# The scan layer's first and last steps: earlier row loads, a first scan inside the convolution, and the last norm, tokens and output products laid into the steps

## The chip, the core and the metric

The kernel runs on one core of one Trainium2 chip. The metric is device time in microseconds (us) from one launch, and smaller is better. Four engines compute: TensorE (PE, with weight loads shown as PEld), VectorE (DVE), ScalarE (ACT) and GpSimd (POOL). Nearly all transfers are issued from SyncE's queue (SP). All data are float32.

## The reference, cut to what matters

Four layers change x (3 images, 256 channels, 48 x 48 pixels), each in the form x + layer(norm(x)), where norm is a group norm over 32 groups. Layer 0 holds attention, layers 1 and 2 are 3 x 3 convolutions, and layer 3 is a selective state-space scan. The change lies between layers 2 and 3 and at the end of layer 3:

```
x = x + conv3x3(group_norm(x))            # layer 2
xn = layer_norm(group_norm(x))            # layer 3, tokens of 256 channels
x_in, z = split(xn @ in_proj.T)           # 512 + 512
u = silu(causal_conv(x_in, 4 taps))
dt_raw, Bm, Cm = split(u @ x_proj.T)      # 16 + 16 + 16
dt = softplus(dt_raw @ dt_proj.T + bias)
h_t = h_(t-1) * exp(dt_t * A) + dt_t * u_t * Bm_t    # 512 x 16 states
y_t = sum_n(h_t * Cm_t) + u_t * D
x = x + (y * silu(z)) @ out_proj.T
```

## The kernel before, in words

**Layer 2.** `output` takes one half image and one half of its channels. PE makes six products (`products`, L1546), ACT copies some of them (L1562), DVE combines them and adds them to the image in SBUF (L1564 to L1576). The images are taken in the order 2, 1, 0, so image 0 (tile x0) is written last, and its very last write is one L1576 on DVE. Finished halves are copied by ACT into token order and stored to DRAM (`store_tokens`, L1642 and L1649), since layer 3 takes its chunks from there. The group norm of a finished image is made in small steps (`next_norm`, `norm_steps`, L183 to L195, L216 to L218, L1614). Beside this the generator `early_preparation` already prepares layer 3's chunk 0 and part of chunk 1: one step of it runs after each product. It ends with dt and dt*u of chunk 0 stored to DRAM (`keep_dt`, L1353 and L1355), and z projected (L1359, L1367).

**Layer 3.** The tokens are cut into 18 chunks of 384 (six for each image). A chunk takes 8 steps, (m, h) for m = 0..3 and h = 0, 1, so there are 144 steps. A step holds eight scans of 128 x 385 on DVE (`scan`, L1819), in parts 0 to 7; each one runs along the tokens. What a step needs:

- dt and dt*u spread over the partitions: `spread` (L1714) and `spread_second` (L1722) reload them from DRAM on SP in groups of four DMAs; `spread_pe` (L1730) spreads two rows by PE into PSUM (ps_r).
- the decays exp(dt*A): `decay` (L1811), one ACT instruction for each scan, into three PSUM slots in turn (ps_da), so ACT can be three scans ahead.
- the products dt*u*B that the scan runs over, in tile hs: the upper half by DVE (`fill_upper`, L1765, from ps_r), the rest by POOL (`fill`, L1780 and L1785).
- after the scans POOL multiplies by C (`times_c`, L1836, 128 x 3072; in the last step DVE does it in two halves, L1830), PE adds the states (`add_states`, L1848 and L1853), and after two steps of an m DVE multiplies by silu(z) (`gate`, L1860).

`run` lays the preparation of the next two chunks and the output of the chunk before (`project_y` L1372 and L1374, `store` L1384 and L1385) between the scans at places given by tables. `keep_busy` (L1336) puts idle 128 x 128 products on PE. From the line `mark` on, `keep_order` fixes the written order on PE, DVE, ACT and POOL. SP's order is left to the scheduler.

**The two ends.** At the start, after layer 2's pools are closed, the code loads the first rows (`spread`, `spread_second`, `spread_pe` for chunk 0), copies the first states (L1794), fills, makes three decays and goes into the loop. Before that, DVE makes the four `diag` matrices (L1704), three memsets (L1748), and the last image's statistics and norm. At the end, after the loop, the residual is loaded, `project_y` adds the residual and m = 0..2, then the last states are added, the last gate is made, the products of m = 3 are added, and ACT copies both halves for two stores.

Of the kernel before, what the change touches and what calls it, by code (L numbers as in the profile page):

```python
# [9 lines left out]
F32 = mybir.dt.float32  # L10
I32 = mybir.dt.int32
AF = mybir.ActivationFunctionType
# [72 lines left out]
def net(  # L85
# [36 lines left out]
    def v(name, i=0, n=1):  # L122
        at = VEC_AT[name] + i
        return vec[:, at : at + n]
# [1254 lines left out]
    def residual(k):  # L1379
        k.ot = room(k, "ot")  # L1380
        nc.sync.dma_start(k.ot, xd[k.b][:, :, k.c * CH : (k.c + 1) * CH])

    def store(k, mo):
        nc.scalar.copy(k.ot[:, mo, :], k.y_out[mo])  # L1384
        nc.sync.dma_start(  # L1385
            out[k.b, mo * P : (mo + 1) * P, k.c * CH : (k.c + 1) * CH], k.ot[:, mo, :]
        )
# [68 lines left out]


    def early_preparation():

# [58 lines left out]
        for m in (0, 2):  # L1518
            project_dt(k, m)
            yield  # L1520
            softplus(k, m)
            yield
            take_dt(k, m)
            yield
            keep_dt(k, m)
            yield
        for m in (0, 2):
            for j in range(2):
                project_z(k, m + j, j)
            yield  # L1530
            for j in range(2):
                take_z(k, m + j, j)
            yield


    with ExitStack() as l1:
# [46 lines left out]
        def moments(b):  # L1583
# [17 lines left out]
            return mv  # L1601

        def next_norm(layer, b):

            last = layer and b == ORDER[-1]
            known = None if last else moments(b)
            for _ in range(9):
                yield
            _, sc, sh = yield from group_norm_steps(b, pss, "s", known=known)
            if layer == 0:  # L1610
                norms[b] = sixth(sc, sh)
            else:
                keep = const.tile([P, 2, CT], F32, name=f"norm3{b}")
                nc.vector.tensor_copy(keep[:, 0, :], sc)  # L1614
                nc.vector.tensor_copy(keep[:, 1, :], sh)
                norm3[b] = keep[:, 0, :], keep[:, 1, :]
# [13 lines left out]
        def store_tokens(b, h):  # L1630


            last = (b, h) == (ORDER[-1], 1)
            if last:
                t = vp.tile([P, 6, CT, (HR + 2) * TW], F32, name="vt")
                t = t.rearrange("p i t n -> p (i t n)")
            else:
                t = pad.tile([P, 4, CT * (HR + 2) * PW + 2], F32, name="xpad")
                t = t.rearrange("p j n -> p (j n)")
            t = t[:, : CT * 4 * HN].rearrange("p (t n) -> p t n", t=CT)  # L1640
            for ct in range(CT):
                nc.scalar.copy(  # L1642
                    t[:, ct, :].rearrange("p (n j) -> p j n", j=4),
                    xs[b][:, ct, :].rearrange("p (j n) -> p j n", j=4)[
                        :, :, h * HN : (h + 1) * HN
                    ],
                )
            queue = nc.scalar if last else nc.sync
            queue.dma_start(xd[b][:, :, h * 4 * HN : (h + 1) * 4 * HN], t)  # L1649
            stored.add((b, h))  # L1650
# [3 lines left out]
        for n, (k, h) in enumerate(halves):  # L1654
# [7 lines left out]
            for m in range(2):  # L1662
                output(b, h, m, u, vt, v("l2_bias", 0, 2) if layer else None)
                for _ in range(13):
                    next(beside.get(k, iter(())), None)
                if m == 0 and behind is not None:
                    store_tokens(*behind)
                    behind = None
# [3 lines left out]
            if h == 1:  # L1672
# [3 lines left out]
                next(pending)  # L1676
        store_tokens(*behind)
        for _ in pending:
            pass
        for _ in early:  # L1680
# [8 lines left out]
    with ExitStack() as l3:  # L1689
        wp = l3.enter_context(tc.tile_pool(name="w3", bufs=1, reuse_waits="tile"))  # L1690
        psd = l3.enter_context(tc.tile_pool(name="psd", bufs=1, space=PSUM))
        psr = l3.enter_context(tc.tile_pool(name="psr", bufs=1, space=PSUM))
        psy = l3.enter_context(tc.tile_pool(name="psy", bufs=1, space=PSUM))

        scn = l3.enter_context(tc.tile_pool(name="scn", bufs=2, reuse_waits="tile"))
        for name in ("u", "dtu", "bc0", "bc1", "sz"):
            rooms[name].append(wp.tile([P, 4, CH], F32, name=name))
# [4 lines left out]
        diag = wp.tile([P, DI, P], F32, name="diag")  # L1702
        for m in range(DI):
            nc.vector.tensor_scalar(diag[:, m, :], ident, v("D", m), None, ALU.mult)  # L1704

# [39 lines left out]
        parts_of_step = [(g, q) for a in range(2) for g in range(2) for q in (2 * a, 2 * a + 1)]  # L1745
        slots = [psd.tile([P, 512], F32, name=f"ps_da{i}") for i in range(3)]
        for t in slots:
            nc.vector.memset(t[:, :1], 0.0)  # L1748

        def states(s):  # L1750

            if s not in tiles:
                t = scn.tile([P, 2, 4, CH + 4], F32, name="hs", bufs=3)
                tiles[s] = t[:, :, :, 1 : CH + 2]
            return tiles[s]
# [15 lines left out]
        def fill(s):  # L1771

            at, m, h = steps[s]
            if h == 0:
                fill_upper(s, 0, 2)
                fill_upper(s + 1, 0, 1, 1 if m == DI - 1 else 2)
            else:
# [45 lines left out]
        def times_c(s):  # L1823
            at, m, h = steps[s]
            cb = chunks[at].bc[1][:, 2 * h : 2 * h + 2, :].unsqueeze(2)
            hc = scn.tile([P, 2, 4, CH], F32, name="hc")
            if s == len(steps) - 1:
# [34 lines left out]
        mark = listed[-1]  # L1862
        last = len(todo) - 1
        k = chunks[0]
        k.rows = {0: spread(k, 0)}
        spread_second(k, 0)
        spread_pe(k, 0)
        first_states(0)
        fill(0)
        for n in range(3):  # L1870
            decay(n)
        for s, (at, m, h) in enumerate(steps):
            if m == 0 and h == 1 and at + 2 <= last:
                fetch(at + 2)
            for part in range(8):
                j = 4 * m + 2 * h + part // 4
                scan(s, part)
                decay(8 * s + part + 3)
                if (m, h, part) in busy:
                    g, q = parts_of_step[part]  # L1880
                    keep_busy(tiles[s][:, g, q, 1 : P + 1], busy[m, h, part])
                if part == 0 and h == 0:
# [6 lines left out]
                if part == 4 and s + 1 < len(steps):  # L1889
                    first_states(s + 1)  # L1890
                if part % 4 == 0:
                    run(at, j, BEGIN)
                if part % 4 == 1:
                    run(at, j, MID)
                if part % 4 == 2:
                    run(at, j, DONE)
                if h == 1 and part == 7 and s >= 3:
                    gate(*steps[s - 3][:2])
# [4 lines left out]
            if s + 1 < len(steps):  # L1903
                fill(s + 1)
            last_states(s)
            times_c(s)
# [6 lines left out]

        end = len(steps) - 1
        k = chunks[last]
        residual(k)
        for mo in range(2):
            project_y(k, mo, 0, DI - 1)
        add_states(end)
        gate(*steps[end][:2])  # L1920
        for mo in range(2):
            project_y(k, mo, DI - 1, DI)
            store(k, mo)
        keep_order(tc, listed, mark)
# [113 lines left out]
```

## Time and profile before

| what | value |
|---|---|
| median of 3 runs | 3367.3 us (3366.03 to 3369.35) |
| the profiled execution's own time | 3369.11 us |
| its span, first to last instruction | 3367.4 us |
| granted TensorE clock over the span | 0.978 |
| busy PE, DVE, ACT, POOL | 3159.9, 2892.8, 2376.1, 1346.1 us |
| last layer 2 product begins | 2008.68 us, its last write on DVE at 2011.79 us |
| first scan begins | 2022.25 us |
| last scan ends, last copy of the output ends | 3344.68 us, 3359.48 us |

Times in the text are microseconds from the start of the span of the one profiled execution. A row such as "L1819 DVE ... xN | busy, mean ns" names a source line, its engine, the operation and how often it ran. The chain of waits follows the work that ended last back from the end, so a wait on it is time that counts; a wait off it may cost nothing.

### The profile page before, as it was taken

What the parts mean: (1) busy time and instruction counts of PE and PEld (TensorE: products, weight loads), DVE (VectorE), ACT (ScalarE), POOL (GpSimd) and SP (SyncE); (2) the same over time, 40 slices, a digit from 0 to 9 for tenths busy, and PEclk for the clock granted to TensorE, in tenths of its full rate; (3) what the DMA queues carried; (4) which work ended last, traced back from release to release, by engine and by line L of the source; (5) the groups of instructions that cost most, each with busy time, mean ns of one, the idle gap of its engine ahead of it and who ended that gap; (6) DMA issues with size and microseconds to landing.
All of it is one profiled execution on the core that took longest, in us unless ns stands there. A gap on an engine that the chain in (4) does not pass through costs nothing.

```text
span 3367.4 us, 54979 instructions
## 1 busy us (share of the span) xinstructions
PE 3159.9 (94%) x21314; PEld 1591.0 (47%) x21314; DVE 2892.8 (86%) x3302; ACT 2376.1 (71%) x3596; POOL 1346.1 (40%) x457
## 2 busy tenths in 40 slices
PE   7999999999999999979999997999999999999995
PEld 4334343352333434547777763444444444444442
DVE  3799989958989998369975459999999999999997
ACT  2688888838888886331324447888888888888874
POOL 0000000000000000220000009999999999999997
PEclk9999999999999999989999999999999999999987
DMA  4000000010000002566611135455555555555552
GB/s 165 31 8 10 8 8 6 8 46 5 8 7 8 10 8 71 174 217 216 216 31 38 38 105 122 120 125 131 134 130 140 135 127 128 133 127 137 133 133 56
DMA packets 182164, 290.84 MB, mean 86 GB/s; under 512 B 34737, under 2 KB 148465, under 8 KB 179970
## 3 DMA queue, kind: packets, MB, share of 16 engines
q1 hardware_dynamic: 168658, 267.15, 29.4%
q10 hardware_dynamic: 13232, 20.06, 1.8%
q8 instruction: 169, 2.77, 0.4%
q14 instruction: 105, 0.86, 0.1%
HBM read 236.24 MB, written 50.64 MB: 85 GB/s over the span
## 4 chain that ended last, share of the span: by engine, by line
PE 52%; DVE 32%; ACT 7%; DMA 5%; issue 4%; SPq 1%; POOL 0%; ACTq 0%; DVEq 0%; POOLq 0%
DVE hs L1819 21%; PE ps_s L638 16%; PE acc L651 14%; PE ps_c L1546 8%; DVE hs L1765 3%; PE ps_s L1031 2%; DVE u L296 2%; PE ps_y L462 2%; ACT ps_da L1811 2%; PE ps_m L665 1%; PE ps_m L711 1%; PE acc L529 1%; PE ps_s L518 1%; DVE ps_g L1343 1%; PE ps_s L578 1%
## 5 line engine op out<-in xcount | busy, mean ns | idle before, releaser
L642 ACT ACTIVATE pt<-ps_s 128x1024 f32<-128x1024 f32 x972 | 942.5, 1022 | 154.6 <-PE ps_s L638 142.1
L1819 DVE TENSOR_TENSOR_SCAN hs<-ps_da,hs 128x385 f32<-128x385 f32 x1152 | 1002.1, 935 | 4.2 <-ACT ps_da L1811 1.5
L857 DVE TENSOR_TENSOR part<-part,pt 128x2048 f32<-128x2048 f32 x396 | 906.6, 2289 | 41.2 <-ACT pt L642 18.4
L1811 ACT ACTIVATE ps_da<-dtr,u 128x384 f32<-128x384 f32 x1152 | 656.6, 582 | 184.3 <-DVE hs L1819 175.7
L164 POOL TENSOR_TENSOR rstd<-ve,mhalf 128x2 f32<-128x2 f32 (+1 forms) x26 | 16.3, 629 | 1480.3 <-DVE ve L162 1480.3
L638 PE MATMUL ps_s<-q,kt 32*128 32x512 f32 (+1 forms) x4320 | 576.4, 592 | 0.1
L651 PE MATMUL acc<-pt,vt 128*32 128x512 f32 (+1 forms) x4320 | 520.9, 561 | 0.2
L1546 PE MATMUL ps_c<-vt,u 128*128 128x288 f32 x1728 | 432.4, 411 | 20.6 <-DVE u L263 20.6
L1836 POOL TENSOR_TENSOR hc<-hs,x 128x3072 f32<-128x3072 f32 x72 | 405.3, 5629 | 19.2 <-DVE hs L1819 15.2
L1836 POOL TENSOR_TENSOR hc<-hs,bc 128x3072 f32<-128x3072 f32 x71 | 399.9, 5633 | 15.9 <-DVE hs L1819 14.2
L1546 PEld LDWEIGHTS ps_c<-vt,u 128*128 128x128 f32 x1728 | 330.8, 192 | 117.1 <-issue 19.4
L638 PEld LDWEIGHTS ps_s<-q,kt 32*128 32x128 f32 x4320 | 195.2, 183 | 199.1 <-issue 120.2
L651 PEld LDWEIGHTS acc<-pt,vt 128*32 128x32 f32 x4320 | 94.4, 108 | 353.4 <-issue 326.7
L1853 PE MATMUL ps_y<-hc,u 128*32 128x384 f32 x2304 | 230.4, 521 | 2.8 <-POOL hc L1836 2.8
L1273 PE MATMUL ps_g<-u 128*128 128x384 f32 x576 | 195.2, 491 | 23.5 <-ACT u L1269 23.5
L1785 POOL TENSOR_TENSOR hs<-dtur,x 128x1536 f32<-128x1536 f32 x72 | 209.2, 2905 | 9.1 <-DMA dtur<-dtud 8.5
L1785 POOL TENSOR_TENSOR hs<-dtur,bc 128x1536 f32<-128x1536 f32 x72 | 209.3, 2907 | 1.1 <-DMA dtuq<-dtud 1.1
L1273 PEld LDWEIGHTS ps_g<-u 128*128 128x128 f32 x576 | 108.3, 191 | 107.2 <-ACT u L1269 34.7
L1336 PE MATMUL ps_r<-hs,ident 128*128 128x128 f32 x864 | 130.7, 292 | 19.8 <-DVE hs L1819 19.5
L1336 PEld LDWEIGHTS ps_r<-hs,ident 128*128 128x128 f32 x864 | 107.6, 192 | 73.8 <-DVE hs L1819 56.1
L1853 PEld LDWEIGHTS ps_y<-hc,u 128*32 128x32 f32 x2304 | 62.4, 113 | 145.0 <-issue 129.6
L1562 ACT COPY cb<-ps_c 128x288 f32<-128x288 f32 x48 | 19.2, 399 | 157.5 <-PE ps_c L1546 137.9
(266 smaller groups left out, 4062.8 us busy)
## 6 DMA issues: line engine op xcount, KB each, us to landing
wconv<-in_we SPq DMA_DIRECT2D x144, 384.0 KB, 4.4
dtr<-dtd SPq DMA_DIRECT2D x288, 192.0 KB, 3.9
dtur<-dtud SPq DMA_DIRECT2D x288, 96.0 KB, 4.2
wconv<-xd SPq DMA_DIRECT2D x36, 384.0 KB, 3.7
x<-bcd SPq DMA_DIRECT2D x72, 192.0 KB, 5.0
dtd<-x SPq DMA_DIRECT2D x36, 384.0 KB, 2.9
dtuq<-dtud SPq DMA_DIRECT2D x288, 48.0 KB, 2.0
bc<-bcd SPq DMA_DIRECT2D x72, 192.0 KB, 4.9
```

The source lines that it names most:

```text
L638: nc.tensor.matmul(s[:, j, cols], kt[r, mt * P : (mt + 1) * P], q[r, :n], start=True, stop=True,)
L642: nc.scalar.activation(p[:, h0 : h0 + 2, :], s, AF.Exp)
L651: nc.tensor.matmul(acc[h * HD : (h + 1) * HD, :n], vt[:, mt, g * P + h * HD : g * P + (h + 1) * HD], p[:, h, cols], start=mt == 0, stop=mt ...
L857: ): nc.vector.tensor_tensor(part, first, p, ALU.add)
L1273: nc.tensor.matmul(bank[m % 2], w3v["taps"][:, m, tap, :], w3v["xi"][:, m % 3, tap : tap + CH], start=tap == 0, stop=tap == DCONV - 1,)
L1336: nc.tensor.matmul(spread_tiles[-1][:, i % 2, CH:], ident, src, start=True, stop=True)
L1546: nc.tensor.matmul(pc[:, :HN], u[:, i, dy, ct, m * P : (m + 1) * P], vt[:, i, ct, dy * TW : dy * TW + HN], start=ct == 0 and dy == 0, stop ...
L1785: nc.gpsimd.tensor_tensor(states(s)[:, :, 2:4, 1:], chunks[at].rows[m][1].unsqueeze(1).broadcast_to([P, 2, 2, CH]), b_rows(s, 0, 2), ALU.mult,
L1811: nc.scalar.activation(slots[n % 3][:, 1 : CH + 1], chunks[at].rows[m][0][:, q, :], AF.Exp, scale=amat[:, col : col + 1],)
L1819: nc.vector.tensor_tensor_scan(b, slots[(8 * s + part) % 3][:, : CH + 1], b, 0.0, ALU.mult, ALU.add)
L1836: nc.gpsimd.tensor_tensor(hc, tiles[s][:, :, :, 1:], cb.broadcast_to([P, 2, 4, CH]), ALU.mult)
L1853: nc.tensor.matmul(k.y_ps[32 * q : 32 * q + 32, :CH], fold, hc[:, g, q, :], start=False, stop=h == 1 and g == 1,)
```

## The change

- **First rows.** A new function `first_rows`, called by `early_preparation` after the last `keep_dt`, issues sixteen DMAs for chunk 0, m = 0: the rows for POOL and the two rows for DVE's fill go into the two xg buffers (SBUF instead of PSUM), dt goes into the dt buffer. The `spread`, `spread_second` and `spread_pe` that stood at the layer's start are gone.
- **First fill and scan.** DVE's last write of layer 2 gets an order dependency on the first scan, so that the first fill and scan stand ahead of it. The three memsets of the decay slots become ACT copies of one column; the slots lie in pools of their own. The second part of the first fill (`fill_upper(1, 0, 1)`) moves behind scan 1 (part 1).
- **Last norm.** `last_norm` replaces the general norm for image 0. Its statistics stay with the image; its PE and DVE steps stand in step 0 at parts 1, 3, 4, 6 and its end, and its last two DVE operations behind scan 1 of step 1. In the built order the 128 x 2 DVE operation ahead of scan 7 of step 0 waits for a PE product that stands behind three `keep_busy` groups, the four products of `project_x` and a fourth group.
- **Last tokens.** The last half image is copied by ACT in pieces into the ot and sq buffers and stored from there on SP: two pieces before layer 2 ends, three within step 0 after parts 0, 2 and 4.
- **diag** is made by ACT, one matrix in every second part of step 1.
- **SP.** Fetches and residual loads that stood among the last transfers of layer 2 come later, since their buffers are in use.
- **keep_busy** runs three products behind parts 1 to 5 of step 0 and parts 4 to 7 of the last step.
- **The end.** The residual is loaded in the last step but one. The last step holds `project_y` for m = 0, 1 at part 0, the gate of m = 2 after scan 3 and then `project_y` for m = 2. After the loop come the last states, the last gate, and the products of m = 3; ACT copies the first output half and DVE the second.

In the built program the order on DVE at the start is: statistics of image 0, fill (L1765), scan 0, last write of layer 2 (L1576), statistics, scan 1, fill, scans 2 and 3, four 128 x 2 operations of the norm, scans 4 to 6, one more, scan 7, fill, and in step 1 scans 0 and 1, the last two norm operations, scans 2 to 7.

The diff at its core:

```diff
+    def last_tokens():
+        a, c = rooms["ot"]
+        return (
+            (0, 0, 192, a.rearrange("p t n -> p (t n)")),
+            (0, 192, HN, c[:, 0, :]),
+            (1, 0, 96, c[:, 1, :]),
+            (1, 96, HN, rooms["sq"][0].rearrange("p t n -> p (t n)")),
+        )
+
+    def copy_tokens(ct, lo, hi, t):
+        nc.scalar.copy(
+            t.rearrange("p (n j) -> p j n", j=4),
+            xs[ORDER[-1]][:, ct, :].rearrange("p (j n) -> p j n", j=4)[
+                :, :, HN + lo : HN + hi
+            ],
+        )
+
+    def store_copied(ct, lo, hi, t):
+        nc.sync.dma_start(xd[ORDER[-1]][:, ct, 4 * (HN + lo) : 4 * (HN + hi)], t)
...
+    def first_rows(k):
+        a, c = rooms["xg"]
+        k.ps, k.second[0] = a, a[:, 1, :]
+        k.rows = {0: (room(k, "dt"), c)}
+        for i in range(4):
+            r = slice(32 * i, 32 * i + 32)
+            nc.sync.dma_start(c[r], k.dtud[0][32:, 0, :].rearrange("(q d) n -> d q n", d=32))
+        for i in range(4):
+            r = slice(32 * i, 32 * i + 32)
+            nc.sync.dma_start(a[r, 0, :], k.dtu[:32, 0, :])
+            nc.sync.dma_start(a[r, 1, :], k.dtud[0][:32, 0, :])
+        for i in range(4):
+            r = slice(32 * i, 32 * i + 32)
+            nc.sync.dma_start(
+                k.rows[0][0][r], k.dtd[0][:, 0, :].rearrange("(q d) n -> d q n", d=32)
+            )
...
+        first_rows(k)
...
+        def last_norm(b):
...
+            ve = small.tile([P, 2], F32, name="ve")
+            nc.vector.tensor_scalar(ve, ps[:, :CT], 1e-5, None, ALU.add)
+            yield
+            r = small.tile([P, 2], F32, name="rstd")
+            nc.gpsimd.tensor_tensor(r, ve, mhalf, ALU.pow)
+            yield
+            keep = const.tile([P, 2, CT], F32, name=f"norm3{b}")
+            nc.vector.tensor_copy(keep[:, 0, :], r)
+            nc.vector.scalar_tensor_tensor(keep[:, 1, :], gm, -1.0, r, ALU.mult, ALU.mult)
+            norm3[b] = keep[:, 0, :], keep[:, 1, :]
...
+                if (b, h, m) == (ORDER[-1], 1, 0) and layer:
+                    for ct, lo, hi, t in last_tokens()[:2]:
+                        copy_tokens(ct, lo, hi, t)
+                        store_copied(ct, lo, hi, t)
...
-        store_tokens(*behind)
-        for _ in pending:
-            pass
+        last_write = next(i for i in reversed(listed) if i.engine == mybir.EngineType.DVE)
+        for _ in range(9):
+            next(pending)
...
-            nc.vector.tensor_scalar(diag[:, m, :], ident, v("D", m), None, ALU.mult)
+        def diagonal(m):
+            nc.scalar.activation(diag[:, m, :], ident, AF.Copy, scale=v("D", m))
...
-                fill_upper(s + 1, 0, 1, 1 if m == DI - 1 else 2)
+                if s:
+                    fill_upper(s + 1, 0, 1, 1 if m == DI - 1 else 2)
...
-        k.rows = {0: spread(k, 0)}
-        spread_second(k, 0)
-        spread_pe(k, 0)
+        spread_tiles[:] = [psr.tile([P, 2, 512], F32, name="ps_r")]
         first_states(0)
         fill(0)
-        for n in range(3):
+        for n, t in enumerate(slots):
+            nc.scalar.copy(t[:, :1], zero[:, :1])
...
+                n = busy.get((m, h, part), 0)
+                if (s == 0 and 1 <= part <= 5) or (s == end and part >= 4):
+                    n = 3
+                if n:
                     g, q = parts_of_step[part]
-                    keep_busy(tiles[s][:, g, q, 1 : P + 1], busy[m, h, part])
+                    keep_busy(tiles[s][:, g, q, 1 : P + 1], n)
+                if s == end and part == 0:
+                    for mo in range(2):
+                        project_y(chunks[at], mo, 0, 2)
+                if s == end and part == 3:
+                    gate(at, DI - 2)
+                    for mo in range(2):
+                        project_y(chunks[at], mo, 2, DI - 1)
+                if s == end - 1 and part == 0:
+                    residual(chunks[at])
...
+                if s == 0:
+                    if part == 0:
+                        scanned = next(
+                            i for i in reversed(listed) if i.engine == mybir.EngineType.DVE
+                        )
+                        tc.add_manual_dep(
+                            last_write, scanned.name,
+                            mybir.DependencyInfo(
+                                mybir.DependencyClass.NoSync, mybir.DependencyReason.DATA
+                            ),
+                            reason="order",
+                        )
+                    if part == 1:
+                        fill_upper(1, 0, 1)
+                    if part in (1, 3, 4, 6):
+                        next(pending)
+                    if part in (0, 2, 4):
+                        ct, lo, hi, t = late_copies[part // 2]
+                        copy_tokens(ct, lo, hi, t)
+                    if part == 5:
+                        for copied in last_tokens()[2:]:
+                            store_copied(*copied)
+                if s == 1:
+                    if part % 2 == 0:
+                        diagonal(part // 2)
+                    if part == 1:
+                        next(pending)
...
-        end = len(steps) - 1
         k = chunks[last]
-        residual(k)
-        for mo in range(2):
-            project_y(k, mo, 0, DI - 1)
         add_states(end)
         gate(*steps[end][:2])
         for mo in range(2):
             project_y(k, mo, DI - 1, DI)
-            store(k, mo)
+        for mo in range(2):
+            store(k, mo, (nc.scalar.copy, nc.vector.tensor_copy)[mo])
```

## The prediction

> **What bounds the kernel now.** I read the page first: its costliest groups say which engine sets a step of the scan layer.
>
> ```profile
> L1819 DVE TENSOR_TENSOR_SCAN hs<-ps_da,hs 128x385 f32<-128x385 f32 x1152 | 1002.1, 935 | 4.2 <-ACT ps_da L1811 1.5
> L1811 ACT ACTIVATE ps_da<-dtr,u 128x384 f32<-128x384 f32 x1152 | 656.6, 582 | 184.3 <-DVE hs L1819 175.7
> ```
>
> DVE sat idle for 4.2 us before 1152 scans and ACT waits for it: inside the layer DVE is the bound, so the change must win at the two ends. Then the chain of waits, cut around the first scan:
>
> ```profile
> 2008.84 2.92 PE ps_c L1546 x12
> 2011.79 0.47 DVE x L1576
> 2012.28 2.29 ACT vt L1642
> 2014.59 6.69 DMA xd<-vt
> 2021.30 2.12 DMA dtur<-dtud
> ...
> 2026.69 1.82 DVE hs L1819 x2
> ```
>
> Each line gives start and length. From the last write (2011.79) to scan 0 (2022.25 in the timeline) the chain is a token copy, its store, and the loads behind them. Last, the chain at the end:
>
> ```profile
> 3344.67 0.46 DVE sz L1860
> ...
> 3346.82 2.72 PE ps_y L1853 x16
> 3349.54 1.25 PE ps_g L1372 x2
> 3350.79 1.94 PE ps_g L1374 x6
> ...
> 3355.30 1.47 PE ps_y L1853 x16
> 3356.80 0.57 DVE sz L1860
> 3357.41 1.57 PE ps_g L1374 x4
> 3359.00 0.48 ACT wconv L1384
> ```
>
> PE makes the output products of m = 0..2 (3349.54 to 3355.30) ahead of the last states, though only the last states depend on the last scans.
>
> [...] seen in the groups by line:
>
> ```profile
> L349 DVE TENSOR_TENSOR wc<-xpad x12: 797/803/2296, 1496.3 to 1939.0; 128x624 f32<-128x624 f32 x12
> L354 DVE SCALAR_TENSOR_TENSOR vt<-vt,wc x12: 795/802/2290, 1501.6 to 1940.4; 128x624 f32<-128x624 f32 x12
> L1830 DVE TENSOR_TENSOR hc<-hs,bc x2: 1745/2482/3220, 3345.0 to 3348.2; 128x1536 f32<-128x1536 f32 x2
> ```
>
> The three numbers are min/median/max in ns. The slow L349 and L354 are the ones that begin inside POOL's L1041 (1496.03 and 1501.19); the slow L1830 (3345.05 to 3348.27) begins inside L1836, which ends at 3346.64. [...] (first number after the length: PE busy):
>
> ```profile
> 2015.71:2019.12 3.41, 0.98 (x4) 0.22 (x2) 2.20 (x5) 1.44 (x2) 0.54 (x1) 1.00 1.08 302
> 2019.12:2022.54 3.42, 0.00 (x0) 0.00 (x0) 1.17 (x2) 1.44 (x3) 0.00 (x0) 0.50 0.47 183
> ...
> 3336.67:3340.08 3.41, 2.79 (x16) 0.60 (x16) 3.41 (x5) 2.15 (x4) 3.41 (x3) 0.50 0.01 2
> 3340.08:3343.50 3.42, 0.00 (x0) 0.00 (x0) 3.42 (x5) 1.86 (x4) 3.42 (x2) 1.00 0.01 2
> ```
>
> The third number from the end is the clock: 29% busy halves the next stretch, 82% restores it.
>
> **Start: when scan 0 can run.** Dt and dt*u of m = 0 left at 1979.5 to 1980.3 (L1353, L1355). The sixteen new DMAs stand on SP behind the second pair (1995.3 to 1996.1 now; 0.2 later, since two token copies replace one). One issue costs 0.44 (1.74 for four L1714). In the built order each also waits for the transfer eight before it, 4 us, so I put the sixteen at 1996.4 to 2004.8 and the last landing at 2008.9 (3.9 for dtr). DMA was idle from 2000 to 2012, so this is hidden; it would show only if over 0.9 late, because ACT is busy with z (L1367) until 2009.36. The sixteen replace twelve at the layer's start, so nothing is late behind them; the fetches that moved feed chunk 2, a whole chunk (74 us) away. After L1367 ACT does the state copy 0.2, a slot copy 0.2, the table load 1.28 and a decay 0.58: 2011.6. DVE has filled by then (four statistics until 2008.8, fill 1.75 with SBUF inputs, POOL idle). Scan 0 at 2011.65 instead of 2022.25: 10.6 won.
>
> **Start: what step 0 gives back.** One scan costs 0.87 in a row (3.50 for four, overlapped). Scan 0 ends at 2012.55; the moved write 0.4, statistics 0.5 and 0.3; scan 1 ends at 2014.65. The next fill has two SBUF inputs; POOL's second L1785 runs from about 2012.7 (L1780 needs the last product) to 2015.6. It ends at 2016.4. Scans 2 and 3: 2018.15. Four 128x2 operations at 0.2: 2018.95. Scans 4 to 6: 2021.65. The next 128x2 operation waits for PE. PE was idle after 2011.75, [...]; three keep_busy products are six passes of 0.127, twice that when halved. Groups 2 and 3 then end at 2020.35; project_x is eight passes of 0.325, or 0.65 [...]; a fourth group 0.75: 2023.8 to 2025.6. I take 2024.9, a stall of 3.2. Scan 7 ends at 2025.95, the third fill at 2026.45. DVE issues it directly behind scan 7, ahead of POOL's L1836, as now (2030.11 against 2030.34). So L1836 runs from 2026.4 to 2032.0 (5.63).
>
> **Start: step 1.** Scans 0 and 1 end at 2028.2. Then the last two norm operations: the second (gm and rstd) has two SBUF inputs, [...] 3.8 us for a 0.15 operation, and six scans stand behind it. [...] I take 3.8. Six scans: 2037.2. Step 1 ends now at 2038.65 (last scan 2037.71 + 0.93), with a 1.09 wait for ACT in it, which the stall covers. The start wins **1.4** (0.5 to 2.4 by the clock). Four diag copies on ACT (0.39 each, L1174) and three token copies (0.8 each, by 2.28 for 1152 columns) lie under these stalls; with the stalls gone they would cost up to 1. DVE's own diag and memsets lay under the load wait and win nothing.
>
> **End.** In today's times: the states of step 141 end on PE at 3339.54. Then the output products of m = 0, 1 (twelve passes: two at 0.65, ten at 0.325) end at 3344.1, m = 2 (its gate, 0.45, is only moved, at 3341.7) at 3345.4, twelve keep_busy products (24 passes of 0.127) at 3348.45, diag 0.65, states 142 1.5, states 143 1.5: 3352.1, where both halves of L1830 are in (3349.94). The clock can move it from 3350.75 to 3353.2. Now: 3356.73 (3355.23 + 1.50). The gate, four passes and copies follow as now; DVE's copy saves nothing, since ACT's two already lie 0.64 apart, behind PE. The end wins **4.6** to 4.9; with the clock's spread 3.5 to 6.0. I take 4.9, the middle.
>
> **Sum.** 1.4 + 4.9 = 6.3. Against the profiled execution's 3369.11 (span 3367.4 and 1.7 around it): 3362.8. It ran 1.8 above the median, so against 3367.3 I forecast 3361.0. About 0.2% (6.7 us) is what a measurement of this kernel can tell from no change; the forecast sits just inside.
>
> **Rivals.** (B) The tiny operation isn't held. Then step 1 ends near 2034 with ACT's and PE's waits, 4.7 won, or 7.5 where PE also stays warm: 9.6 to 12.4 in all, 3356.5. For it: no trace of so small an operation. Against: two operations on DVE, tensor_tensor and scalar_tensor_tensor alike, waited. (C) [...] 2.9 more, 3363.9. For it: L1785 starts at L1836's end (2035.93 against 2035.97). Against: held L1830 went on within 0.1 of POOL's end. (D) Slower: PE's clock stays halved through the whole last step, since the new order puts about 11 us of products ahead of the last states. Price: eight output products 10.4, keep_busy 6.1, diag 1.3, states 2 x 2.79, from 3339.54: 3363.0, 6.3 later than now, 1.0 more for the last four passes, less the start's 1.4: 3373.2. It decides only if the clock is still halved past about 3348. Against: one stretch at 82% restored it. That the change does not act (rows late, scan 0 as late as now) needs DMAs 10 us late with DMA idle; under 1 in 50, counted in C.
>
> **How the numbers follow.** Forecast A 0.50 (3358.9 to 3363.3; a little under half of it past the 6.7 us), B 0.27, C 0.17, D 0.06. Faster by over 0.2%: 0.23 of A and all of B, 0.50. Within 0.2%: 0.27 of A and C, 0.44. Slower: D, 0.06. The range reaches into B and C: 3355 to 3364.5 leaves out D, B's tail and C's, near 0.17.
>
> **What would show it.** Scan 0 near 2011.6 against the last product; a DVE gap of 2 to 4 us ahead of scan 7 of step 0 put down to PE; a gap near 3.8 us behind scan 1 of step 1 that ends with L1836; step 1's end about 1.4 earlier; last states 4 to 6 closer behind the last scan. Without the second gap B is right; with a gap past 6, C. If scan 0 stands near 2013 or later, the sixteen DMAs were mis-sized.

## The result, and the profile after

| | before | after |
|---|---|---|
| median, first comparison (8 runs each) | 3366.7 us | 3355.7 us (3349.8 to 3359.5) |
| ratio, 95% interval | | 0.9964 [0.9953, 0.9975] |
| profiled execution, its span | 3369.11, 3367.4 us | 3359.47, 3357.7 us |
| last sum of layer 2 on DVE (L1564, L1602) to the first scan | 18.4 us | 7.6 us |
| end of the last scan to the end of the last copy | 14.8 us | 9.0 us |

By its median the kernel became 11.0 us faster, 0.33%; the ratio gives 0.36%, with an interval of 8.4 to 15.8 us. The forecast was 6.3. Its direction was right, and 3355.7 lies in its range, but the size was not right.

The costliest groups of the scan layer on the page of the kernel after (those of before stand in the prediction):

```profile
L1897 DVE TENSOR_TENSOR_SCAN hs<-ps_da,hs 128x385 f32<-128x385 f32 x1152 | 1003.5, 940 | 2.8 <-ACT ps_da L1889 1.3
...
L1889 ACT ACTIVATE ps_da<-dtr,u 128x384 f32<-128x384 f32 x1136 | 648.9, 584 | 177.1 <-DVE hs L1897 169.3
```

DVE stays the bound inside the layer: it sat idle for 2.8 us before the 1152 scans, 4.2 before. So the gain is to be looked for at the ends. The chain of waits at the start (start, length, what):

```profile
2003.33 4.00 DMA x<-dtd
...
2007.62 1.28 ACT L1889
2008.92 0.59 ACT ps_da L1889
2009.54 0.96 DVE hs L1897
2010.49 0.36 DVE x L1614
...
2012.60 2.52 DVE hs L1842
...
2016.05 2.93 PE ps_r L1336 x12
2018.98 3.44 PE ps_g L1263 x8
...
2023.09 0.13 PE ps_y L1661 x2
2023.24 0.16 DVE ve L1664
```

Scan 0 no longer waits for a token store and its loads. It waits for ACT's table load (1.28) and a decay. The last DMA of the first rows landed at 2007.33, 0.3 ahead of the table load. Behind scan 0 the chain shows what was paid: the last write (L1614), the fill L1842 with 2.52, and then PE: twelve keep_busy passes, eight of project_x and six more of keep_busy stand ahead of the two passes of L1661, for which DVE's `ve` (the variance of the last norm) waits. The chain at the end:

```profile
3342.38 2.68 PE ps_r L1336 x24
3345.06 0.65 PE ps_y L1926 x2
3345.70 2.76 PE ps_y L1931 x32
...
3348.49 0.57 DVE sz L1938
...
3349.10 1.57 PE ps_g L1374 x4
...
3350.70 0.56 DVE wconv L1384
```

Sixteen passes of the states of step 142 and sixteen of step 143 now run in one piece of 2.76 us, behind keep_busy, and only the gate, four passes and a copy follow. Before, sixteen passes of output products lay between them. PE's queue bounds this end: in the chain it runs from 3333.88 to the last state product without a pause.

### The profile page after: what moved, and what is told of

It reads as the page before. It is cut to its first block, busy times and chain, and to the rows that moved or that the text cites. A ratio compares the mean times of both kernels' runs of the same rounds, so it can differ in the third digit from the quotient of the medians.

```text
span 3357.7 us, 55087 instructions
## 1 busy us (share of the span) xinstructions
PE 3158.8 (94%) x21364; PEld 1596.5 (48%) x21364; DVE 2898.4 (86%) x3294; ACT 2379.8 (71%) x3605; POOL 1348.2 (40%) x457
## 4 chain that ended last, share of the span: by engine, by line
PE 53%; DVE 31%; ACT 7%; DMA 4%; issue 4%; POOL 1%; SPq 1%; ACTq 0%; DVEq 0%; POOLq 0%
DVE hs L1897 20%; PE ps_s L638 16%; PE acc L651 14%; PE ps_c L1584 7%; DVE hs L1842 3%; PE ps_s L1031 2%; DVE u L296 2%; PE ps_y L462 2%; PE ps_m L665 2%; ACT ps_da L1889 2%; PE ps_m L711 1%; PE acc L529 1%; PE ps_s L518 1%; DVE ps_g L1343 1%; PE ps_g L1359 1%
## 5 line engine op out<-in xcount | busy, mean ns | idle before, releaser
L857 DVE TENSOR_TENSOR part<-part,pt 128x2048 f32<-128x2048 f32 x396 | 906.7, 2290 | 41.2 <-ACT pt L642 18.4
L1889 ACT ACTIVATE ps_da<-dtr,u 128x384 f32<-128x384 f32 x1136 | 648.9, 584 | 177.1 <-DVE hs L1897 169.3
L1914 POOL TENSOR_TENSOR hc<-hs,bc 128x3072 f32<-128x3072 f32 x71 | 399.7, 5630 | 15.8 <-DVE hs L1897 13.8
L1273 PE MATMUL ps_g<-u 128*128 128x384 f32 x576 | 194.9, 491 | 12.3 <-ACT u L1269 12.3
L1336 PE MATMUL ps_r<-hs,ident 128*128 128x128 f32 x918 | 139.8, 294 | 27.3 <-DVE hs L1897 27.1
L1336 PEld LDWEIGHTS ps_r<-hs,ident 128*128 128x128 f32 x918 | 115.6, 194 | 81.9 <-DVE hs L1897 63.2
L1273 PEld LDWEIGHTS ps_g<-u 128*128 128x128 f32 x576 | 108.3, 191 | 95.3 <-ACT u L1269 22.9
```

The lines of the kernel that those rows point to most:

```text
L857: ): nc.vector.tensor_tensor(part, first, p, ALU.add)
L1273: nc.tensor.matmul(bank[m % 2], w3v["taps"][:, m, tap, :], w3v["xi"][:, m % 3, tap : tap + CH], start=tap == 0, stop=tap == DCONV - 1,)
L1336: nc.tensor.matmul(spread_tiles[-1][:, i % 2, CH:], ident, src, start=True, stop=True)
L1889: nc.scalar.activation(slots[n % 3][:, 1 : CH + 1], chunks[at].rows[m][0][:, q, :], AF.Exp, scale=amat[:, col : col + 1],)
L1914: nc.gpsimd.tensor_tensor(hc, tiles[s][:, :, :, 1:], cb.broadcast_to([P, 2, 4, CH]), ALU.mult)
```

## The experiments

Each kernel is timed against the kernel before on the same chip. Intervals in us are those of the ratio, taken of the kernel before. Where a text says "layer start" it means: from the last sum of layer 2 on DVE (L1564 before, L1602 after) to the first scan of step 3. The stretches of one profiled execution of each, all in us:

| kernel | load | first convolution | layer start | step 3 to last copy | behind last copy | median (runs) |
|---|---|---|---|---|---|---|
| before | 116.5 | 451.9 | 45.1 | 1310.5 | 7.9 | 3366.3 (112, all runs) |
| before_again | 114.5 | 449.1 | 46.2 | 1311.3 | 8.2 | 3364.6 (13) |
| sp_shift | 115.7 | 450.0 | 46.0 | 1311.1 | 6.3 | 3363.9 (21) |
| warm_end | 116.4 | 456.2 | 46.3 | 1313.5 | 7.8 | 3367.8 (13) |
| start_only | 115.4 | 445.5 | 43.8 | 1309.2 | 6.3 | 3360.9 (21) |
| end_only | 115.7 | 445.3 | 44.9 | 1305.2 | 7.3 | 3359.3 (8) |
| after | 114.9 | 451.6 | 44.0 | 1305.4 | 6.5 | 3355.7 (8) |
| after_again | 116.1 | 448.9 | 43.8 | 1305.0 | 6.3 | 3357.1 (7) |
| no_busy_end | 116.0 | 449.0 | 43.7 | 1304.4 | 6.3 | 3356.3 (11) |
| copies_on_act | 114.6 | 451.7 | 44.1 | 1304.3 | 6.2 | 3357.2 (13) |
| product_early | 116.0 | 449.5 | 40.7 | 1304.8 | 7.0 | 3355.0 (5) |
| norm_on_act | 114.0 | 448.7 | 39.9 | 1304.3 | 6.7 | 3351.8 (5) |
| both | 116.2 | 452.3 | 40.0 | 1304.5 | 6.3 | 3354.3 (5) |
| both_warm | 114.6 | 453.0 | 38.2 | 1305.2 | 6.0 | 3351.0 (5) |

"Load" ends where the first L857 starts (DVE's sums in the attention), "first convolution" runs from the start of the last L857 to that of the first L1573 (L1611 after), and "step 3" begins with its first scan. Not listed: the attention between (1204.6 to 1205.2 in all) and the second convolution (230.5 to 230.6 in all). The table is read by columns: a column that moves with the edit is the edit's, and one that moves within the same kernel is scatter. Load and first convolution move by 2.5 and 10.9 us in whatever order, though no edit touches them.

### One part of the change alone

`end_only`, the kernel before with

```diff
+                if s == end and part >= 4:
+                    n = 3
...
+                if s == end and part == 0:
+                    for mo in range(2):
+                        project_y(chunks[at], mo, 0, 2)
+                if s == end and part == 3:
+                    gate(at, DI - 2)
+                    for mo in range(2):
+                        project_y(chunks[at], mo, 2, DI - 1)
+                if s == end - 1 and part == 0:
+                    residual(chunks[at])
...
```

and without the lines behind the loop that these replace; the second of the last copies is on DVE.

> The kernel before, with only the end of the change: output products, the gate of m = 2, the fetch of the residual and four times three keep_busy products moved into the last step, the last copy on DVE. Theory 1 (the ends as profiled, the rest scatter): in the profiles before and after the wait of the last gate behind the last hc shrank by 5.4 us (8.31 less 2.88), so 5 to 5.5 us faster than before, about 3361.3 against 3366.7. Theory 2 (the end is worth more on average than in that one profile): 8 to 9 us faster, about 3358. Theory 3 (the missing 4.4 us lie outside both ends, in the first 80 us or in the program's last instructions, and come with any change of the code): 5.4 plus up to 3.4, and the profile shows the offset before 1950 us.

Measured: 3359.3 us, ratio 0.9981 [0.9970, 0.9991], which is 3.0 to 10.1 us. From step 3 to the last copy 1305.2 instead of 1310.5: 5.3. Theory 1's size fits. The median alone does not exclude theory 2, but no stretch shows 8 us. An offset as in theory 3, before 1950 us, is there too (7.7), 6.6 of it in the first convolution; whether it comes with the build is the next question.

`start_only`, the kernel after with those lines taken out and the old end put back:

> The kernel after, with the end of the change undone (output products, gate, residual and both copies as in the kernel before, no keep_busy products in the last step). Theory 1: step 1 ends 1.2 to 1.4 us earlier against the layer's last product and nothing else changes: 3365.3 against 3366.7. Theory 2: the same, 3365.3. Theory 4 (the start is worth more on average than in the profiled pair, because the stalls ahead of scan 7 and behind scan 1 differ from run to run): 5 to 6 us faster, 3361.

Measured: 3360.9 us, 0.9982 [0.9976, 0.9989], 3.7 to 8.1 us: too much for theory 1. But the layer start won only 1.3 (43.8 against 45.1), and in the five executions with this start it moves by no more than 0.4 (43.7 to 44.1), so theory 4 falls too: the rest is outside the steps that the start changes. The column behind the last copy shows a part of it: 6.3 against 7.9, in a kernel whose end is written as before.

### Is it the build or the execution?

`before_again` and `after_again` are the two kernels unchanged.

> The kernel before once more, unchanged. Asks which stretches of its first profile are its own and which were one execution's. Theory 1 (scatter): the stretch of the first convolution (451.9 us from the last attention operation to the last convolution's middle; 445.3 to 451.6 in the other five profiles) and the load stretch (116.5; 114.0 to 116.0) move by some us, the second half of the convolution (230.6), the layer's start (45.1) and the scans (1295.7) do not move, the stretch from the last scan to the last copy (14.8) moves by up to 1.2 with PE's clock. Theory 3 (each build has its own fixed costs): 116.5, 451.9 and 14.8 come again within 0.5, and the pause of 1.5 us in SP's last instructions (from 3364.7 to 3366.2, 1.3 us in the kernel with the end alone, none in the four kernels with the changed start) comes again. Median 3366.5 either way.

Measured: 3364.6 us, 0.9993 [0.9984, 1.0001]. Load and first convolution did not come again (116.5 and 451.9 became 114.5 and 449.1); what lies behind the last copy did, 8.2. So both theories hold a part: scatter in the first two columns, and a fixed cost of the build in the last. The layer start, which was expected to stay, moved by 1.1 as well (46.2). The fixed cost is read from SP's ten closing semaphore instructions (one row: engine, count, ns min/median/max, first to last start). The second run of the kernel before:

```profile
L2034 SPq EVENT_SEMAPHORE  x10: 17/28/28, 3362.0 to 3364.9; - x10
```

The kernel after:

```profile
L2152 SPq EVENT_SEMAPHORE  x10: 17/28/28, 3356.4 to 3357.7; - x10
```

They take 2.9 us before and 1.3 after, though none is longer than 0.03: between two of them SP pauses for 1.5 us (1.50 and 1.55 in the two executions of the kernel before).

> The kernel after once more, unchanged. If the 11.0 us of the first comparison (8 runs) were partly scatter, the median moves toward the sum of the ends, 1.2 + 5.4 + the 1.5 of SP's last pause + the clock's 0.5: 3358 to 3359. If the two parts as measured alone (7.1 and 5.5) are true, it stays at 3354 to 3356. Its stretches: layer start 44.0, last scan to last copy 9.0, from there to the end 6.3 to 7.0 without SP's pause.

Measured: 3357.1 us, 0.9968 [0.9957, 0.9980]. The fifteen runs of the kernel after have a median of 3355.9, against 3366.3 for before: 10.4.

`sp_shift`, the kernel before with

```diff
-        nc.sync.dma_start(
-            out[k.b, mo * P : (mo + 1) * P, k.c * CH : (k.c + 1) * CH], k.ot[:, mo, :]
-        )
+        n = 4 if 1 <= k.at <= 4 else 1
+        for i in range(n):
+            r = slice(i * P // n, (i + 1) * P // n)
+            nc.sync.dma_start(
+                out[k.b, mo * P : (mo + 1) * P, k.c * CH : (k.c + 1) * CH][r], k.ot[r, mo, :]
+            )
```

> The kernel before, with the output stores of chunks 1 to 4 cut into four DMAs of 32 rows each, so that 24 more DMA instructions stand on SP's queue long before the end, off every chain of waits. If the pause of 1.5 us in SP's last instructions belongs to the place where they stand in its stream, it is gone or lies elsewhere: 1.5 us faster in the last stretch, 3365.0. If it belongs to the layer's end as built before, it stays: 3366.5. No theory gives more than 1.5.

Measured: 3363.9 us, 0.9994 [0.9987, 1.0000]. The row of SP's closing instructions:

```profile
L2037 SPq EVENT_SEMAPHORE  x10: 17/28/28, 3363.0 to 3364.2; - x10
```

1.2 us: the pause is gone, with 24 more instructions on SP more than 900 us earlier, and nothing else changed. The stretch is 6.3 instead of 7.9 and 8.2. The counts of SP's instructions recorded in the traces fit: 2292 in the three kernels that pause (the kernel before, `end_only`, `warm_end`), 2299 in all that have the new start, 2316 here. So the pause hangs on the place of these instructions in SP's stream, and the changed start, which alters their number, removed it by chance. That it is the place, the runs show; what makes SP pause there, they do not.

### The two stalls at the start

`norm_on_act`, the kernel after with

```diff
-            nc.vector.tensor_copy(keep[:, 0, :], r)
-            nc.vector.scalar_tensor_tensor(keep[:, 1, :], gm, -1.0, r, ALU.mult, ALU.mult)
+            nc.scalar.copy(keep[:, 0, :], r)
+            for ct in range(CT):
+                nc.scalar.activation(
+                    keep[:, 1, ct : ct + 1], keep[:, 1, ct : ct + 1], AF.Copy,
+                    scale=r[:, ct : ct + 1],
+                )
```

where step 0 had put the negative mean into `keep[:, 1, :]`. What it removes, in the timeline of the kernel after (start, length, engine, line):

```profile
2024.50 5.71 POOL L1914 TENSOR_TENSOR hc<-hs,x 128x3072 f32<-128x3072 f32 x1 [0.32 <-DVE hs L1897]
...
2026.35 3.88 DVE L1670 COPY norm<-rstd 128x2 f32<-128x2 f32 x1
...
2030.15 0.15 DVE L1671 SCALAR_TENSOR_TENSOR norm<-gm,rstd 128x2 f32<-128x2 f32 x1
2030.17 2.90 POOL L1863 TENSOR_TENSOR hs<-dtur,x 128x1536 f32<-128x1536 f32 x1
```

A copy of 128 x 2, from SBUF to SBUF, begins at 2026.35 with its input ready (rstd was made from 2023.48 in 0.69) and ends when POOL's hc (the states times C) does: 3.88 us. A copy of the same shape elsewhere (L1689) takes 0.17. Either POOL's operation held the copy, or the copy waited for something else.

> The kernel after, with the last two norm operations (the copy of rstd and the product of the mean with it) on ACT instead of DVE, which leaves nothing small on DVE inside POOL's 5.7 us hc of step 0; the sign of the mean is turned by one more small DVE operation in step 0. [...] the gap behind scan 1 of step 1 is gone in the profile, and 3 to 3.8 us are won against the kernel after (about 3352.4), less where the scans then wait for ACT, which fills the gap with decays today: 2 at the least. If the copy waited for something else (rstd from POOL, or the order on DVE), ACT waits in its place, the decays stand behind it, and nothing is won: 3355.7.

Measured: 3351.8 us, 0.9956 [0.9943, 0.9970]; the layer start 39.9, 4.1 less than 44.0. So POOL's operation held the copy, not a wait for rstd and not the order on DVE. DVE's waits between 2009 and 2042 us of this kernel (in total, times, longest):

```profile
DVE ve L1666 <- PE ps_y L1663: 2.8, 1, 2.8
DVE hs L1902 <- ACT ps_da L1894: 0.7, 1, 0.7
```

The gap behind scan 1 is gone, the one at `ve` stays.

`product_early`, the kernel after with

```diff
-                    if part in (1, 3, 4, 6):
-                        next(pending)
+                    for _ in range({1: 1, 3: 2, 6: 1}.get(part, 0)):
+                        next(pending)
```

> The kernel after, with the second small norm product put on PE ahead of project_x and of two groups of keep_busy products instead of behind them. If the 3.18 us gap ahead of scan 7 of step 0 is PE's queue, it goes: 2.5 to 3.2 us won in step 0. What is won there moves POOL's hc and the held copy forward by the same amount, so it should last to step 1's end: 3352.5 to 3353.2 against 3355.7. If another stall takes its place (the decay for scan 7, or the project_x copies on ACT ahead of it), under 1 us: 3355.

Measured, DVE's waits in the same window:

```profile
DVE hs L1897 <- ACT ps_da L1889: 1.3, 2, 0.7
```

The wait at `ve` is gone from DVE's waits, and the layer start is 40.7: 3.3 less, where 2.5 to 3.2 was expected. The median, 3355.0 (0.9966 [0.9952, 0.9979]), shows little of it: single runs scatter by some 2 to 3 us, and five of them can't tell 3.3 from 1.

`both` puts the two edits together.

> The kernel after, with both edits at the start together: the second small norm product ahead of project_x on PE, and the last two norm operations on ACT. In the profiles the layer's start took 44.0 us with the change, 39.9 with the norm operations on ACT (4.1 less) and 40.7 with the product early (3.3 less). If the two stalls are separate, 7.4 less: 36.6, and a time of 3348.3. If the scans then catch up with ACT's decays (0.58 each, three small norm operations of 0.2, four diag copies of 0.39 and three token copies of 0.88 stand among them), a third stall takes 1 to 3 us of it: 38 to 39, 3350 to 3351.

Measured: 3354.3 us, 0.9960 [0.9946, 0.9974]; layer start 40.0, no less than with the norm on ACT alone (39.9). A third stall took all that the second edit won (0.63 of the 4.0 lie ahead of scan 0):

```profile
DVE hs L1902 <- ACT ps_da L1894: 4.0, 5, 1.6
```

In its timeline the wait of 1.62 goes back, through a decay, to an activation on ACT that waits for the products of the causal convolution on PE (L1273), which follow those of project_x (L1263):

```profile
2025.42 5.33 PE L1273 MATMUL ps_g<-u 128*128 128x384 f32 x16
...
2030.79 0.58 ACT L1281 ACTIVATE u<-ps_g,vec 128x384 f32<-128x384 f32 x1 [1.53 <-PE ps_g L1273]
2031.27 0.58 ACT L1894 ACTIVATE ps_da<-x,u 128x384 f32<-128x384 f32 x1
...
2031.88 0.96 DVE L1902 TENSOR_TENSOR_SCAN hs<-ps_da,hs 128x385 f32<-128x385 f32 x1 [1.62 <-ACT ps_da L1894]
```

`both_warm` is `both` with more keep_busy products:

```diff
-                if (s == 0 and 1 <= part <= 5) or (s == end and part >= 4):
-                    n = 3
+                if (s == 0 and part <= 5) or (s == end and part >= 4):
+                    n = 9 if s == 0 and part <= 1 else 3
```

> The kernel with both edits at the start, and PE kept busy there: nine keep_busy products of two passes each behind scans 0 and 1 of step 0 (none and three before). In the kernel with both edits the layer's start took 39.98 us, no less than with the norm operations on ACT alone (39.89), and the scans of step 1 waited 0.27 + 0.50 + 1.62 us for ACT, whose decays stand behind an activation that waited for project_x's second products on PE (16 passes in 5.33 us, twice their full-speed time, behind eight in 3.38). If PE's halved clock is that third stall, those 24 passes take 8.71 - 4.3 = 4.4 us less, the waits in step 1 go, and the layer's start takes 37.6 to 38.2: 1.8 to 2.4 us less. If the stall is ACT's own work or the order of its instructions, the start stays at 39.9; and if the added products (36 passes by 0.127 = 4.6 us at full clock, 30 of them new) hold up the small norm products, it gets longer by up to 2.

PE's stretches behind the last product, in the kernel after (the third number from the end is the clock):

```profile
2012.00:2015.40 3.40, 1.05 (x8) 0.97 (x8) 3.40 (x3) 0.80 (x2) 2.31 (x1) 0.75 1.02 218
2015.40:2018.80 3.40, 2.75 (x13) 2.75 (x14) 3.29 (x8) 2.17 (x4) 0.00 (x0) 0.50 0.43 105
```

and in `both_warm`:

```profile
2012.00:2015.40 3.40, 3.40 (x32) 3.38 (x31) 3.37 (x4) 1.79 (x3) 3.18 (x1) 1.00 1.00 237
2015.40:2018.80 3.40, 2.51 (x22) 2.31 (x21) 3.30 (x9) 1.78 (x3) 0.00 (x0) 1.00 0.64 156
```

The clock stays full, the eight passes of L1263 take 2.85 instead of 3.38, and the layer start is 38.2, 1.8 less. One part of the expectation was wrong: the sixteen passes of L1273 take 5.33 at full clock as well, so these products only started earlier and did not get shorter. DVE still waits for ACT, 2.7 instead of 4.0 (0.96 of it ahead of scan 0):

```profile
DVE hs L1902 <- ACT ps_da L1894: 2.7, 3, 1.0
```

At 3351.0 us, 0.9961 [0.9947, 0.9974], it is the fastest by its median, 4.7 below the first median of the kernel after, though the intervals of the two ratios overlap; the runs do not tell it from `norm_on_act` (3351.8) either.

### The end: which engine bounds it

`no_busy_end`, the kernel after with

```diff
-                if (s == 0 and 1 <= part <= 5) or (s == end and part >= 4):
+                if s == 0 and 1 <= part <= 5:
```

> The kernel after, without the twelve keep_busy products of the last step (24 passes, 2.84 us on PE). The forecast had PE as the bound of the last step: then PE is 2.84 us ahead and the last scan to the last copy takes up to 2.8 us less than 9.0, less what a halved clock takes back. If DVE's last two hc operations (4.90 us, the second ends at 3347.07, 1.35 ahead of PE's last state product) are the bound now, at most 0.5 us is won: 8.5 to 9.0, and 3355.5 in all. If the products keep the clock at full speed and are needed for that, the sixteen last state products, diag and four output passes take up to twice their time: 10 to 11 us, 3357.

Measured: 3356.3 us, 0.9975 [0.9966, 0.9984]; from the last scan to the last copy 8.5 us. Freed of 2.84 us PE did not end 2.8 earlier; its last eight passes wait for DVE:

```profile
3339.64 4.88 DVE L1908 TENSOR_TENSOR hc<-hs,bc 128x1536 f32<-128x1536 f32 x2
...
3344.58 0.85 PE L1931 MATMUL ps_y<-hc,u 128*32 128x384 f32 x8 [0.81 <-DVE hc L1908]
3345.50 0.56 DVE L1938 TENSOR_TENSOR sz<-ps_y,sz 128x384 f32<-128x384 f32 x1 [0.98 <-PE ps_y L1931]
```

So without those products DVE's two hc operations (4.88) and what follows them are the limit. In the kernel after PE's queue still ends last, but its 9.0 is within 0.5 of that limit. The clock, full from 3335.87 on here (two passes of L1372 took 1.65 before and 0.81 after), did not need the keep_busy products.

`copies_on_act`, the kernel after with `store(k, mo, nc.scalar.copy)`:

> The kernel after, with both last copies on ACT as in the kernel before. In the profile of the kernel after ACT's copy lies at 3350.05 (0.48 long) and DVE's at 3350.70 (0.56), behind PE's pass for it. On ACT the second would start at 3350.69 as well: no difference, within 0.1 us in the last stretch (9.0); the forecast put the DVE copy at nothing. A rival: ACT, free sooner, ends 0.1 to 0.3 earlier because its copy is the shorter one.

Measured: 3357.2 us, 0.9972 [0.9964, 0.9981]; last scan to last copy 8.5, as in the other executions in which PE was ahead (8.54 to 8.55; here its clock was full: 23 recorded keep_busy passes in 2.73 us, as 24 in 2.84 in the kernel after), less 0.08 for the shorter copy. The DVE copy is worth nothing, as forecast.

`warm_end`, the kernel before with

```diff
+                if s == len(steps) - 1 and part >= 4:
+                    n = 6
```

> The kernel before, with nothing of the change but PE kept busy in the last step: six keep_busy products of two passes each behind each of scans 4 to 7. Asks how much of the end's gain (last scan to last copy 14.8, 15.3, 15.3 and 13.8 us with the old end, 8.5 to 9.0 with the new) is PE's clock and how much the order of the products. In the second profile of the kernel before PE ran from 3341.9 to about 3348 at half speed: diag 1.65, sixteen state products 2.79, the first products of the output 3.95 in place of 0.81, 1.50 and 2.8, so the clock costs it 3.3 us, of which diag's 0.8 lies ahead of the wait for hc. If clock and order share the gain so, the end takes 12.0 to 12.8 and the kernel runs 2 to 3 us faster than before: 3363.5 to 3364. If the order is all of it, 14 or more and 3366. The products behind scan 7 (12 passes, 1.5 us) end before the hc of step 142 does and cost nothing.

Measured: 3367.8 us, 1.0004 [0.9996, 1.0012]: not faster, and the end 17.5 us instead of 14.8. The expectation failed because the 48 passes took 8.37 us, where twice the 2.84 of 24 passes at full clock in the kernel after is 5.68, and the diag product stood behind them. The difference fits a clock that was halved for about the first 23 passes, an estimate from these two figures:

```profile
3347.57 8.37 PE L1336 MATMUL ps_r<-hs,ident 128*128 128x128 f32 x48 [3.54 <-DVE hs L1819]
3355.78 0.81 PE L1848 MATMUL ps_y<-u,diag 128*128 128x384 f32 x2
```

But from the first state product to the last PE then took 8.28 us at full clock (3356.52 to 3364.80; the first sixteen state products took 1.50, not the 2.79 that they took at a clock of 0.50 in the first profile of the kernel before). In the second run of the kernel before, where that began at half clock, it took 10.47 (3343.51 to 3353.98). Diag, ahead of it, ran at half clock too (1.65 instead of 0.81), but the state products could not have begun sooner, since POOL's hc ended at 3343.40:

```profile
3337.76 5.64 POOL L1836 TENSOR_TENSOR hc<-hs,bc 128x3072 f32<-128x3072 f32 x1
...
3341.93 1.65 PE L1848 MATMUL ps_y<-u,diag 128*128 128x384 f32 x2 [6.48 <-DVE sz L1860]
3343.51 2.79 PE L1853 MATMUL ps_y<-hc,u 128*32 128x384 f32 x16
```

From these figures the half clock cost the old end an estimated 2.2 us in that run; the same sum gives 1.7 in the first (3346.75 to 3356.73). With PE at full clock the old end would have been about 13.1 us in both (15.3 less 2.2, 14.8 less 1.7), against 9.0 with the new one. So of what the new order wins from the last scan to the last copy about 4 us are the order itself, and about 2 the clock. The keep_busy products don't bring those 2: in `no_busy_end`, with the output products in the step and without keep_busy, the clock was full again from 3335.87 on, ahead of the last four scans.

## Why the prediction was right or wrong

What failed is the term for the end, "The end wins 4.6 to 4.9": up to the last copy it was under-sized (5.3 measured), and behind the last copy, where the sum had nothing, 1.6 were won. The start and its stalls came much as forecast. Some 2 us of the 11.0 remain unexplained.

- **Start, scan 0.** Forecast 2011.65; in the trace 2009.54, and the whole trace runs 1.92 earlier there (last product 2006.76 against 2008.68), so 2011.46. The last of the sixteen DMAs landed at 2007.33, 0.3 ahead of the table load, where 0.9 to spare had been worked out.
- **Start, what step 0 gives back.** The stall at scan 7 was 3.18, forecast 3.2. The second fill took 2.61 and ended 0.82 behind POOL's rows (2014.31): it waited for POOL as forecast, but those rows took 3.44 instead of 2.90, which cost 0.6; why they took longer stays open.
- **Start, step 1.** The tiny operation was held, 3.88 for 3.8, so rival B is out; that its 3356.5 came nearest to the 3355.7 measured is chance. But the copy waited, the first of the two, not the second with its two SBUF inputs. That copy has a single SBUF input and took 3.88 where L1689 took 0.17. The second took 0.15 and began 0.02 ahead of POOL's next operation: that one did not come between the two, as rival C had it (2.9 more), so C is out as well.
- **Start in all.** 1.4 forecast; 1.1 between the two first profiles, and 1.8 between the means of the layer start with the old start (45.1, 46.2, 46.0, 44.9, 46.3) and the new (44.0, 43.8, 43.8, 43.7, 44.1). The right size owes something to luck: the second fill lost 0.6 that the sum did not have, and scan 0 came 0.2 sooner.
- **End, up to the last copy: under-sized.** The step put PE's queue as the bound, with the last state product at 3352.1. PE's queue was the bound, but in the trace that product ended at 3348.42, or 3351.30 by the clock of before (2.88 by the last hc): 5.4 won for 4.6. The sum had carried over the time of step 141's states at half clock; with PE's clock halved only from 3334.67 to 3338.09, they took 2.06 instead of 2.79 (lines below). Over all executions the column gives 5.3 (1310.5 as mean of the four with the old end and without added work, 1305.2 of `after`, `after_again` and `end_only`) to 6.1 where PE was ahead and DVE's hc set the end (1304.4 in `no_busy_end`, `copies_on_act`, `norm_on_act` and `both`; 1305.2 in `both_warm`). Rival D is out: the half clock was over before the last scans. A small slip beside it: the middle of the forecast's 3.5 and 6.0 is 4.75, not 4.9.
- **End, behind the last copy: missed.** "Against the profiled execution's 3369.11 (span 3367.4 and 1.7 around it)": the sum took the 7.9 us behind the last copy as fixed. They hold SP's pause, and it is gone after: 1.6 (mean of 7.9 and 8.2 less mean of 6.5 and 6.3). No step of the forecast aimed at it.

The states of step 141 on PE, in the kernel before and in the kernel after:

```profile
3336.75 2.79 PE L1853 MATMUL ps_y<-hc,u 128*32 128x384 f32 x16 [2.83 <-POOL hc L1836]
```

```profile
3333.88 2.06 PE L1931 MATMUL ps_y<-hc,u 128*32 128x384 f32 x16 [2.83 <-POOL hc L1914]
```

With the measured sizes, 1.8 + 5.3 + 1.6 = 8.7 us in place of 6.3. It lies in both intervals (8.4 to 15.8, and 6.7 to 14.5 of the second comparison). The first comparison's 11.0 holds some 2 us more. No stretch that the edits touch shows them; the first convolution, where the same code takes 445 to 456 us from one execution to the next, can hide them. Load and first convolution together take 566.3 us on average in the five executions with the old start and 565.3 in the nine with the new, too near to tell at that scatter. Whether the 2 us are scatter alone stays open; the same holds for `start_only`, where the layer start (1.9 below the old mean) and the closing pause (1.8) give 3.7 of the 5.4 measured.

## What to carry to other kernels

Read the profile past the last computing instruction: the last microseconds of a program can hold a pause (1.3 to 1.6 us here) that an unrelated edit moves in or out, and a gain or loss of 1 or 2 us in a long kernel can be that. Two stalls in a row aren't added up: removing either one here took 3.3 to 4.1 us off the layer start and removing both took no more, since another engine's queue was close behind. And where DVE is the bound, look for a small copy from SBUF to SBUF inside a long POOL operation: the one here took 3.88 us instead of 0.17, and ACT made the same copy in 0.18.

## What the runs showed of the hardware

- A 128 x 2 copy on DVE with a single SBUF input was held by a POOL operation to its end (3.88 us instead of 0.17).
- SP's closing instructions pause 1.3 to 1.6 us in the kernel before (both executions), `end_only` and `warm_end`, and not in the ten other executions; 24 more DMA instructions on SP far ahead of them removed the pause.
- The same code of the first convolution takes 445.3 to 456.2 us from one execution to the next, while attention and the second convolution hold within 0.6 and 0.1.
